# Order of the score tiles on TensorE in the middle batches of a graph-attention and attention kernel

## The chip, the cores and the metric

The kernel runs on one core of a Trainium2 chip. The time is that of one execution on the device, in microseconds (us), and lower is better. A core has five engines that work side by side, each through its own list of instructions in order: TensorE (PE) for matrix products, VectorE (DVE), ScalarE (ACT) and GpSimd (POOL) for elementwise work, and SyncE (SP), which here issues transfers. They wait for each other by semaphores. [...] 

## The reference

For each of 32 batches, x is 512 nodes by 512 features, in fp32, and `adj` is one 512 x 512 mask for all of them. Layer 0 is a graph attention with one head, layer 1 an attention with 8 heads of 64, each with a residual and a layer norm:

```python
def layer0(X, A, W, a):
    h = einsum('bnf,fo->bno', X, W)                    # 512 x 256 a batch
    e = leaky_relu(h @ a[0] + swapaxes(h @ a[1], 1, 2), 0.2)
    alpha = softmax(e + -1e9 * (1 - A), axis=-1)
    return concatenate([einsum('bij,bjo->bio', alpha, h), h], axis=-1)

def layer1(h, adj):
    q, k, v = (split_heads(h @ W.T + b) for W, b in ((Wq, bq), (Wk, bk), (Wv, bv)))
    s = where(adj == 0, -inf, einsum('bhqd,bhkd->bhqk', q, k) / 8)
    out = einsum('bhqk,bhkd->bhqd', softmax(s), v)
    return join_heads(out) @ Wo.T + bo

x = layernorm(x + layer0(x, adj, W, a))
x = layernorm(x + layer1(x, adj))
```

## The kernel before

**Layout.** One batch's 512 rows are four row tiles of 128. The eight heads are four pairs (`hp` 0 to 3); the two heads of a pair share one 128-partition tile of queries and keys, 64 partitions each, so that TensorE works on both at once, on its upper and lower half. All products are in fp32, and the profile shows two matmul records for each. The large projections (queries and keys: `project_two`, tiles `pw`; values: `project_v`, tiles `pv`; output: `finish_seven`, tiles `pf`) are done with seven products of blocks in place of eight, with sums of the blocks made by VectorE or GpSimd.

**A pair.** `head_scores(b, hp, i)` handles row tile i: two score matmuls into two PSUM tiles `ps` (L701); for each of them VectorE adds the mask and takes the row's maximum in one instruction (`minus_max`, L315, result `p` and `least`), and ScalarE takes the exponential and the row sum (L710). `head_blocks` transposes the eight `p` tiles in 32 x 32 blocks on VectorE into `t` (L330), and `head_move` moves blocks with 16 transfers from `t` to `pt` on SP (L347). In the next pair's time `head_products` multiplies `pt` with the values (tile `pav`, L763), and `head_divide` scales by the row sums (`inv`, fetched by GpSimd's transfers in `head_inverse`) into `ot` (L778).

**What runs around it.** While batch b is in its attention, layer 0 of the next batches is woven in. In `middle_batch(b)`, which handles batches 1 to 29:

- pair 0: the values' projection of b (`project_v`, a generator: its first `next` makes product `pv1` and ScalarE's copy of it, L647; the second the other six, three copies and a sum on GpSimd; the end VectorE's four results `v`, L657); layer 0's scores of b+1 (`l0_scores`: ScalarE's leaky rectifier L455, then the mask on GpSimd, L459), its row (`l0_row`, GpSimd L434; `leaky`, VectorE L417) and its weights (`l0_weights`: subtraction on VectorE L469, exponential on ScalarE L470); the first two products of the output projection of b-1 (`finish_seven`).
- pair 1: layer 0's products `po` of b+1 (L477) with their layer norm, then `project_two(b, 1)`: the queries and keys of pairs 2 and 3 (L547, results `qk` on VectorE L584).
- pair 2: the other five products of the output projection (L802).
- pair 3: layer norm of b-1 (`out_stats` on VectorE, `ln_root` on ScalarE, `out_norm` on both), layer 0's projection of b+2 (`l0_project`, four tiles `ph`, L264, copied by ScalarE) and its columns (`l0_columns`: a copy on ScalarE and two transfers on SP, L389 and L391), `l0_maxima` (four reductions on VectorE over `pn`) with two transfers, the store of b-1, and `project_two(b + 1, 0)` for pairs 0 and 1 of the next batch.

**What sets the order.** Each engine runs its instructions in the order in which the Python code records them. PSUM is two pools of four banks: `ps_s` (scores, `psum_s`) and `ps_m` (everything else, `psum`). A new tile takes a bank whose last readers have been recorded, and waits on the chip until they are done. The `p` tiles share nine SBUF buffers with the copies of the projections, `pn` and `row`. Batches 0, 30 and 31 have a loop of their own.

Of the kernel before, what the change touches and what calls it, by code (L numbers as in the profile page):

```python
# [26 lines left out]
def kernel(  # L27
# [241 lines left out]
    def psum_s(name):  # L269
        return ps_s.tile([P, N], F32, name=name, tag="s")  # L270
# [12 lines left out]
    def ln_root(key, tiles=range(NB)):  # L283
        mv, rstd = st["ln", key]
        lo, hi = tiles[0], tiles[-1] + 1
        nc.scalar.activation(rstd[:, lo:hi], mv[:, lo:hi, 1], AF.Sqrt, bias=eps)
# [84 lines left out]
    def l0_project(b, i):  # L371

        l0_copy(b, i, l0_product(b, i))
# [241 lines left out]
    def project_v(b):  # L615

        x1t, tx = st["x1t", b], st["tx", b]
        half = F // 2

        def product(ps, columns, weights, start=True):  # L620
            for k in range(2):
                for c in range(FC // 2):
                    nc.tensor.matmul(  # L623
                        ps[:, k * half : (k + 1) * half],
                        columns(k, c),
                        weights(c),
                        start=start and k == 0 and c == 0,
                        stop=c == FC // 2 - 1,
                        skip_group_check=True,
                    )  # L630

        def a_(i, f):
            cols = slice(i * half, (i + 1) * half)
            return lambda c: wv_sb[:, 2 * f + c, cols]

        def s_(i):
            return lambda c: wvx_sb[:, i, c, :]

        def b_(f, j):
            return lambda k, c: x1t[:, 2 * j + k, 2 * f + c, :]  # L640

        def t_(i):
            return lambda k, c: tx[:, i, k, c, :]

        def copy(ps, name):
            t = prob.tile([P, N], F32, name=f"{name}_{b}_v", tag="p", bufs=PB)
            nc.scalar.copy(t, ps)  # L647
            return t

        out = []  # L650
        for j in range(2):
            v = act.tile([P, 2, F], F32, name=f"v_{b}_{j}", tag="v", bufs=2)
            st["v", b, j] = v
            out.append(v)

        def result(i, j, ps, other):
            nc.vector.tensor_tensor(  # L657
                out[j][:, :, i * half : (i + 1) * half],
                ps.rearrange("p (k d) -> p k d", k=2),
                other.rearrange("p (k d) -> p k d", k=2),  # L660
                ALU.add,
            )

        b1 = psum(f"pv1_{b}")
        product(b1, b_(0, 0), a_(0, 0))
        p1 = copy(b1, "p1")
        yield
        b3, b4 = psum(f"pv3_{b}"), psum(f"pv4_{b}")
        product(b3, t_(0), s_(0))
        p5 = copy(b3, "p5")  # L670
        product(b4, t_(2), a_(1, 0))
        p7 = copy(b4, "p7")
        nc.gpsimd.tensor_tensor(p7, p7, p5, ALU.add)
        product(b1, t_(1), s_(1), start=False)
        u2 = copy(b1, "u2")
        b2 = psum(f"pv2_{b}")
        product(b2, b_(1, 0), a_(0, 1))
        product(b3, b_(1, 1), s_(2), start=False)
        product(b4, t_(3), a_(1, 1), start=False)
        yield  # L680
        result(1, 1, b1, p7)
        result(0, 0, b2, p1)
        result(0, 1, b3, u2)
        result(1, 0, b4, u2)

    def head_scores(b, hp, i):
        qk = st["qk", b, hp]
        if i == 0:
            if (b, hp) not in turned:
                st["t", b, hp] = prob.tile(  # L690
                    [P, 4, 2, FC, NB, G], F32, name=f"t_{b}_{hp}", tag="t", bufs=1
                )
            st["tot", b, hp] = small.tile(
                [P, 2, NB], F32, name=f"tot_{b}_{hp}", tag="total", bufs=3
            )
        total = st["tot", b, hp]
        pss = []
        for j in range(2):
            rows = slice(j * D, (j + 1) * D)
            ps = psum_s(f"ps_{b}_{hp}_{i}_{j}")  # L700
            nc.tensor.matmul(  # L701
                ps, qk[rows, 0, i * P : (i + 1) * P], qk[rows, 1, :], start=True, stop=True
            )
            pss.append(ps)
        for j in range(2):
            name = f"{b}_{hp}_{i}_{j}"
            p = prob.tile([P, N], F32, name=f"p_{name}", tag="p", bufs=PB)
            least = small.tile([P, 1], F32, name=f"least_{name}", tag="least", bufs=6)
            minus_max(p, pss[j], mask1[:, i, :], least)
            nc.scalar.activation(  # L710
                p, p, AF.Exp, bias=least, scale=-1.0, accum_out=total[:, j, i : i + 1]
            )
            st.setdefault(("p", b, hp), []).append((j, i, p))
# [11 lines left out]
    def head_blocks(b, hp):  # L725
        for j, i, p in st.pop(("p", b, hp)):
            transpose_blocks(st["t", b, hp][:, :, j], i, p)
# [29 lines left out]
    def head_products(b, hp, bank=None):  # L757
        pt = st.pop(("pt", b, hp))
        po = st["pav", b, hp] = (bank or psum)(f"pav_{b}_{hp}")
        for c in range(NB):  # L760
            for j in range(2):
                head = 2 * hp + j
                nc.tensor.matmul(  # L763
                    po[j * D : (j + 1) * D, :],
                    st["v", b, c // 2][:, c % 2, head * D : (head + 1) * D],
                    pt[:, :, j, c, :, :].rearrange("p g i q -> p g (i q)"),
                    start=(c == 0),
                    stop=(c == NB - 1),
                )
# [130 lines left out]
    def out_stats(b):  # L900
        z, key = st["x1", b], f"1_{b}"
        for i in range(NB):
            ln_stats(z, key, i)
# [98 lines left out]
    def middle_batch(b):  # L1002


        seven = finish_seven(b - 1, lambda: load_x(b + 1, nc.gpsimd))
        for hp in range(NP):
            last = (b, hp - 1) if hp > 0 else (b - 1, NP - 1)
            head_scores(b, hp, 0)
            head_scores(b, hp, 1)
            if hp in (1, 2):  # L1010
                head_products(*last)
            if hp == 0:
                values = project_v(b)
                next(values)
                l0_scores(b + 1, [0, 1])
            elif hp == 1:
                next(seven)
                l0_add_h(b + 1)
            elif hp == 2:
                add_bias(b + 1)  # L1020
            if hp < 3:
                head_blocks(b, hp)
            else:
                out_stats(b - 1)
                ln_root(f"1_{b - 1}")
                for i in range(NB):
                    l0_project(b + 2, i)
                l0_columns(b + 2)
            head_scores(b, hp, 2)
            head_scores(b, hp, 3)  # L1030
            if hp == 2:
                next(seven)
            else:
                if hp == 3:
                    out_norm(b - 1)
                if hp != 1:
                    head_products(*last)
            pair_ends(b, hp)
            if hp == 2:
                next(seven)  # L1040
            head_divide(*last)
            if hp == 0:
                l0_row(b + 1)
                l0_scores(b + 1, [2, 3])
                leaky(st["row", b + 1])
                next(values)
                l0_weights(b + 1)
                head_inverse(b, 0)
                steps(values)
                next(seven)  # L1050
                next(seven)
            elif hp == 1:
                l0_output(b + 1)
                load_xt(b + 2)
                two = project_two(b, 1)
                next(two)
                l0_norm(b + 1)
                next(two)
                head_inverse(b, 1)
                blocks = x1_blocks(b + 1)  # L1060
                for part in (blocks, two, blocks, two, blocks):
                    next(part, None)
            elif hp == 2:
                steps(seven)
                x1_sums(b + 1, nc.gpsimd)
                head_inverse(b, 2)
                if b == 1:
                    add_bias(1)
            else:
                l0_maxima(b + 2)  # L1070
                l0_write(b + 2)
                l0_read(b + 2)
                store(b - 1)
                steps(project_two(b + 1, 0))
                head_inverse(b, 3)

    before = None
# [201 lines left out]
```

## Time and profile before

| | |
|---|---|
| median of 3 runs | 3063.42 us (3062.69 to 3063.91) |
| span of the profiled execution | 3060.1 us |
| PE, weight load beside it | 99%, 67% busy |
| DVE, ACT, POOL | 84%, 50%, 42% busy |
| DMA | 151 GB/s mean |
| scores L701 | 2048 records, 510.5 us busy |
| products with the values L763 | 2048 records, 467.7 us busy |
| reductions L315 on scores | 1024, mean 683 ns |
| exponentials L710 | 1024, mean 711 ns |
| block transposes L330 | 992, mean 683 ns |

The span covers the first to the last instruction; the runs' time has some microseconds around it. Instructions of one engine overlap at their ends, so the step from one start to the next is what an instruction costs in a run. A batch repeats every 93.6 us: pair 2 of one batch starts its scores at 1506.76 in the trace, that of the next at 1600.39. In that window pair 3 starts at 1523.22, pair 0 at 1550.09 and pair 1 at 1573.45.

### The profile page before, as it was taken

Reading aid. Unit: us, or ns where it says so; the run is one execution under the profiler, and the core shown is the slowest. Engines: PE = TensorE matmul, PEld = TensorE weight load, DVE = VectorE, ACT = ScalarE, POOL = GpSimd, SP = SyncE. Lnnn points to the kernel's source line nnn. Section 1 sums busy time; section 2 is a strip of 40 time slices with the busy share of each in tenths; the row PEclk is TensorE's granted clock in tenths of the full one; section 3 lists DMA queues with packets and bytes.
Section 4 is the critical chain, followed back from the end, with each engine's and each line's share of the span. In section 5 each row is a group of like instructions: output and inputs, shape, how many; then the busy total and the mean of one; then the engine's idle time right before and its main releaser. Section 6 shows DMA issues by size and latency. Waiting matters only on the chain.

```text
span 3060.1 us, 44716 instructions
## 1 busy us (share of the span) xinstructions
PE 3036.1 (99%) x13492; PEld 2061.2 (67%) x13492; DVE 2565.8 (84%) x5707; ACT 1541.0 (50%) x3264; POOL 1287.2 (42%) x1253
## 2 busy tenths in 40 slices
PE   8999999999999999999999999999999999999998
PEld 6666666666666666666666666666666666666665
DVE  7788888888888888888888888888888888888865
ACT  4454555445554545554455545455544555455544
POOL 4353444443434434444444444344444444343422
PEclk9999999999999999999999999999999999999999
DMA  6456666666665666666666666666666666666642
GB/s 185 115 142 162 154 157 155 150 162 156 152 159 144 160 158 154 158 154 147 169 153 149 159 147 162 154 157 151 157 149 164 159 147 163 147 156 159 156 101 66
DMA packets 237440, 462.53 MB, mean 151 GB/s; under 512 B 94544, under 2 KB 97104, under 8 KB 237200
## 3 DMA queue, kind: packets, MB, share of 16 engines
q1 hardware_dynamic: 216848, 395.42, 54.6%
q0 software_dynamic: 20352, 64.25, 6.7%
q8 instruction: 109, 1.79, 0.3%
q14 instruction: 131, 1.07, 0.1%
HBM read 132.65 MB, written 34.27 MB: 55 GB/s over the span
## 4 chain that ended last, share of the span: by engine, by line
PE 92%; DVE 4%; issue 1%; SPq 1%; POOL 1%; DMA 1%; ACT 0%; ACTq 0%; DVEq 0%; POOLq 0%
PE pw L547 23%; PE ps L701 15%; PE pav L763 14%; PE pf L802 12%; PE pv L623 12%; PE ph L264 7%; PE po L477 7%; SPq L347 1%; DVE t L330 1%; DVE p L315 1%; DVE stats L280 0%; PE pt L741 0%; PE pf L876 0%; DVE x L486 0%; ACT p L710 0%
## 5 line engine op out<-in xcount | busy, mean ns | idle before, releaser
L710 ACT ACTIVATE p<-p,least 128x512 f32<-128x512 f32 x1024 | 726.4, 711 | 664.2 <-DVE least L315 629.4
L315 DVE CUSTOM_DVE_ANT_0 p<-ps,mask 128x512 f32<-128x512 f32 x1024 | 642.9, 683 | 129.8 <-PE ps L701 126.4
L330 DVE STREAM_TRANSPOSE t<-p 128x512 f32<-128x512 f32 x992 | 625.6, 683 | 33.8 <-ACT p L710 12.7
L701 PE MATMUL ps<-qk 64*128 64x512 f32 x2048 | 510.5, 615 | 1.4 <-DVE qk L584 1.1
L763 PE MATMUL pav<-pt,v 128*64 128x512 f32 x2048 | 467.7, 598 | 2.6 <-DMA pt<-t 1.9
L754 POOL DMA_DIRECT2D inv<-d_tot x256 | 134.1, 528 | 747.0 <-DMA d_tot<-tot 318.7
L763 PEld LDWEIGHTS pav<-pt,v 128*64 128x64 f32 x2048 | 136.2, 136 | 318.6 <-issue 291.2
L701 PEld LDWEIGHTS ps<-qk 64*128 64x128 f32 x2048 | 177.2, 186 | 236.6 <-issue 161.8
L825 POOL TENSOR_TENSOR x<-x,u_o 128x512 f32<-128x512 f32 x93 | 115.5, 1269 | 338.3 <-ACT u_o L820 338.2
L825 DVE TENSOR_TENSOR x<-x,pf 128x512 f32<-128x512 f32 x186 | 125.4, 677 | 147.9 <-POOL x L825 90.7
L477 PE MATMUL po<-h,et 128*128 128x257 f32 x1024 | 235.1, 386 | 2.6 <-ACT et L470 2.0
L264 PE MATMUL ph<-w_sb,xt 128*128 128x258 f32 x1024 | 234.5, 386 | 0.3 <-DVE w_sb L190 0.3
L600 POOL TENSOR_TENSOR p<-p,p 128x512 f32<-128x512 f32 x64 | 86.5, 1352 | 352.2 <-ACT p L571 352.1
L477 PEld LDWEIGHTS po<-h,et 128*128 128x128 f32 x1024 | 189.1, 190 | 59.8 <-issue 15.8
L264 PEld LDWEIGHTS ph<-w_sb,xt 128*128 128x128 f32 x1024 | 193.0, 191 | 51.2 <-PE ps L701 22.0
L710 ACT ACTIVATION_READ_ACCUMULATOR p<-p,least 128x1 f32 x1024 | 191.4, 187 | 0.0
L710 ACT ACT_TABLE_LOAD x62 | 79.5, 1283 | 210.1 <-DVE least L315 209.6
L459 POOL TENSOR_TENSOR et<-et,mask0t 128x512 f32<-128x512 f32 x126 | 154.6, 1243 | 73.0 <-ACT et L455 72.5
L280 DVE BATCH_NORM_STATS2 stats<-x 128x6 f32<-128x512 f32 x252 | 171.8, 682 | 13.7 <-DVE x L486 0.9
L802 PE MATMUL pf<-wo_sb,ot 128*128 128x256 f32 x744 | 179.6, 384 | 0.1
L802 PE MATMUL pf<-wox_sb,ot 128*128 128x256 f32 x744 | 176.9, 382 | 0.0
L802 PEld LDWEIGHTS pf<-wo_sb,ot 128*128 128x128 f32 x744 | 138.3, 190 | 44.6 <-issue 25.0
(155 smaller groups left out, 5443.9 us busy)
## 6 DMA issues: line engine op xcount, KB each, us to landing
pt<-t SPq DMA_DIRECT2D x1984, 128.0 KB, 2.4
inv<-d_tot POOLq DMA_DIRECT2D x256, 128.0 KB, 3.6
xt<-in_xt_dram SPq DMA_DIRECT2D x31, 1024.0 KB, 7.5
x1t<-x1t_b SPq DMA_DIRECT2D x496, 64.0 KB, 2.0
out_dram<-x SPq DMA_DIRECT2D x31, 1024.0 KB, 6.9
x<-in_x_dram POOLq DMA_DIRECT2D x29, 1024.0 KB, 5.6
rows<-d_att SPq DMA_DIRECT2D x31, 512.0 KB, 3.8
rows<-d_least SPq DMA_DIRECT2D x31, 256.0 KB, 4.3
```

Source lines behind the costliest of these rows:

```text
L264: nc.tensor.matmul(ps, lhs(c), rhs(c), start=(c == 0), stop=(c == FC - 1))
L280: nc.vector.bn_stats(stats, z[:, i, :])
L315: nc.vector.tensor_tensor_reduce(out=out, in0=scores, in1=mask, scale=-1.0, scalar=MIN_INIT, op0=ALU.add, op1=ALU.min, accum_out=least,)
L330: nc.vector.transpose(t[:, :, :, i, :].rearrange("p r c q -> p c r q"), src.rearrange("p (c r k) -> p c r k", r=4, k=G),)
L477: nc.tensor.matmul(po, et[:, j, i * P : (i + 1) * P], h_sb[:, j, 2:], start=(j == 0), stop=(j == NB - 1),)
L547: nc.tensor.matmul(ps[:, k * half : (k + 1) * half], weights(k, c), moving(c), start=start and k == 0 and c == 0, stop=c == FC // 2 - 1, s ...
L623: nc.tensor.matmul(ps[:, k * half : (k + 1) * half], columns(k, c), weights(c), start=start and k == 0 and c == 0, stop=c == FC // 2 - 1, ...
L701: nc.tensor.matmul(ps, qk[rows, 0, i * P : (i + 1) * P], qk[rows, 1, :], start=True, stop=True)
L710: nc.scalar.activation(p, p, AF.Exp, bias=least, scale=-1.0, accum_out=total[:, j, i : i + 1])
L763: nc.tensor.matmul(po[j * D : (j + 1) * D, :], st["v", b, c // 2][:, c % 2, head * D : (head + 1) * D], pt[:, :, j, c, :, :].rearrange("p ...
L802: nc.tensor.matmul(ps[:, k * half : (k + 1) * half], columns[:, c, k * P : (k + 1) * P], weights(c), start=start and k == 0 and c == 0, st ...
L825: engine.tensor_tensor(to, to, term.rearrange("p (k d) -> p k d", k=2), ALU.add)
```

## The change

In the middle batches only. All four row tiles of a pair's scores are recorded in a row; the last two use banks of `ps_m`, and the product with the values of the pair before follows them, in a bank of `ps_s`. All eight block transposes of a pair come together after that (`head_blocks` is left only in `pair_ends`). The values' first product moves behind that product, and layer 0's scores ahead of its copy. Layer 0's projection of b+2 is split: three of its four tiles go to the end of pair 2, behind the output projection, and the fourth stays in pair 3, behind the product with the values, with `l0_columns` after it. The layer norm of b-1 (`out_stats`, `ln_root`, `out_norm`) moves into `project_two(b + 1, 0)`, between its parts, and `l0_maxima` with its transfers too; the store follows.

```diff
-    def head_scores(b, hp, i):
+    def head_scores(b, hp, i, bank=psum_s):
...
-            ps = psum_s(f"ps_{b}_{hp}_{i}_{j}")
+            ps = bank(f"ps_{b}_{hp}_{i}_{j}")
...
-            head_scores(b, hp, 0)
-            head_scores(b, hp, 1)
-            if hp in (1, 2):
-                head_products(*last)
+            for i in range(NB):
+                head_scores(b, hp, i, psum_s if i < 2 else psum)
+            head_products(*last, psum_s)
             if hp == 0:
                 values = project_v(b)
+                l0_scores(b + 1, [0, 1])
                 next(values)
-                l0_scores(b + 1, [0, 1])
             elif hp == 1:
                 next(seven)
                 l0_add_h(b + 1)
             elif hp == 2:
                 add_bias(b + 1)
-            if hp < 3:
-                head_blocks(b, hp)
-            else:
-                out_stats(b - 1)
-                ln_root(f"1_{b - 1}")
-                for i in range(NB):
-                    l0_project(b + 2, i)
-                l0_columns(b + 2)
-            head_scores(b, hp, 2)
-            head_scores(b, hp, 3)
-            if hp == 2:
                 next(seven)
             else:
-                if hp == 3:
-                    out_norm(b - 1)
-                if hp != 1:
-                    head_products(*last)
+                l0_project(b + 2, NB - 1)
+                l0_columns(b + 2)
             pair_ends(b, hp)
...
             elif hp == 2:
                 steps(seven)
+                for i in range(NB - 1):
+                    l0_project(b + 2, i)
                 x1_sums(b + 1, nc.gpsimd)
...
             else:
+                two = project_two(b + 1, 0)
+                out_stats(b - 1)
+                next(two)
+                ln_root(f"1_{b - 1}")
+                out_norm(b - 1)
+                next(two)
                 l0_maxima(b + 2)
                 l0_write(b + 2)
                 l0_read(b + 2)
+                steps(two)
                 store(b - 1)
-                steps(project_two(b + 1, 0))
                 head_inverse(b, 3)
```

## The prediction

> **What bounds the kernel now.** I read the page's busy shares first, then the chain of waits, then the timeline of one middle batch, engine by engine. TensorE is busy nearly all the time, and the chain that ended last is almost wholly TensorE, so only two things count: how long TensorE's own work takes, and any new idle time on it.
>
> ```profile
> PE 3036.1 (99%) x13492; PEld 2061.2 (67%) x13492; DVE 2565.8 (84%) x5707; ACT 1541.0 (50%) x3264; POOL 1287.2 (42%) x1253
> PE 92%; DVE 4%; issue 1%; SPq 1%; POOL 1%; DMA 1%; ACT 0%; ACTq 0%; DVEq 0%; POOLq 0%
> ```
>
> The timeline of TensorE through pair 0 of a batch. Columns: start in us, duration, engine, line, what, count. Let T0 be the start of pair 0's first scores, here 1550.09.
>
> ```profile
> 1550.09 1.99 PE L701 MATMUL ps<-qk 64*128 64x512 f32 x8
> 1552.01 1.99 PE L623 MATMUL pv<-wv_sb,x1t 128*128 128x256 f32 x8
> 1553.93 1.99 PE L701 MATMUL ps<-qk 64*128 64x512 f32 x8
> 1555.85 3.65 PE L763 MATMUL pav<-pt,v 128*64 128x512 f32 x16
> 1561.27 1.89 PE L623 MATMUL pv<-wv_sb,tx 128*128 128x256 f32 x8
> 1562.99 1.89 PE L623 MATMUL pv<-wvx_sb,tx 128*128 128x256 f32 x8
> 1569.90 1.89 PE L802 MATMUL pf<-wo_sb,ot 128*128 128x256 f32 x8
> 1573.45 1.99 PE L701 MATMUL ps<-qk 64*128 64x512 f32 x8
> ```
>
> Eight records of the values' projection take 1.72 us inside a run (1561.27 to 1562.99), but 1.92 us when they stand alone between scores (1552.01 to 1553.93). The array has three shapes here (64*128 scores, 128*64 product, 128*128 the rest), and a run of one shape costs about 0.20 us over its streaming. A score run shows the same: its inner pairs of matmuls start 0.43 apart, so four pairs stream in 1.72, and the run takes 1.92.
>
> The other engines around the same pair:
>
> ```profile
> 1551.99 0.72 ACT L710 ACTIVATE p<-p,least 128x512 f32<-128x512 f32 x1 [6.38 <-DVE least L315]
> 1555.29 2.40 ACT L455 ACTIVATE et<-rows,h 128x512 f32<-128x512 f32 x2
> 1509.01 1.28 ACT L710 ACT_TABLE_LOAD   x1 [6.69 <-DVE least L315]
> ...
> 1556.62 2.31 POOL L459 TENSOR_TENSOR et<-et,mask0t 128x512 f32<-128x512 f32 x2 [0.63 <-ACT et L455]
> 1558.89 2.19 POOL L434 TENSOR_TENSOR row<-rows 128x512 f32<-128x512 f32 x1
> ...
> 1550.60 0.47 DVE L584 SCALAR_TENSOR_TENSOR qk<-pw,bk_sb,u 128x256 f32<-128x256 f32 x1
> 1551.25 0.69 DVE L315 CUSTOM_DVE_ANT_0 p<-ps,mask 128x512 f32<-128x512 f32 x1 [0.18 <-PE ps L701]
> 1562.60 0.83 DVE L417 SCALAR_TENSOR_TENSOR row<-row 128x512 f32<-128x512 f32 x1
> 1563.46 4.41 DVE L469 TENSOR_TENSOR et<-et,row 128x512 f32<-128x512 f32 x4
> 1567.80 1.28 DVE L657 TENSOR_TENSOR v<-pv,p_v 128x512 f32<-128x512 f32 x2
> ```
>
> Look at the order: four exponentials, two leaky rectifiers (L455), two mask additions on POOL, POOL's row (L434), then VectorE's row, four subtractions (L469) and the values' results (L657). The first output-projection matmul (pf, 1569.90) takes the PSUM bank which the first of those results frees, at about 1568.4. This chain has 1.5 us to spare today, and the change lengthens it.
>
> **What the change removes.** Per middle batch the instruction order has 18 runs of one shape before and 12 after: four score runs merge with others, and two full-shape runs (the values' first product, layer 0's projection) join neighbours. 6 x 0.20 = 1.2 us, times 29 middle batches: 34.8 us. The output projection of pair 2 also holds one inner wait today: its 40 records take 1514.17 to 1523.22, 9.05 us, against 40 x 0.2155 + 0.21 = 8.83. It waits for VectorE's addition of the first product, about 12.6 after the pair's start. After the change that addition ends at about 12.05 and is wanted at 12.5, so I take 0.2 more: 1.4 us a batch.
>
> **What it moves, pair 3 (T3 = its first scores).** Nothing is added to any engine, but orders change. TensorE: scores 16 x 0.215 + 0.19 = 3.63, product 3.59 (1555.85 to 1559.43), the last tile of layer 0's projection 1.84, seven products of 1.724 and a switch: the next T0 is T3 + 21.23. The layer norm's root now stands on ScalarE behind the fourth product's copy. That product ends at T3 + 15.96; 0.2 to the copy, copy 0.58, table load 1.28, root 0.30: T3 + 18.3. VectorE is idle meanwhile and has queued behind it: reciprocal and shift 0.58, four results qk 1.80, four reductions of pn at 0.61, four more qk 1.76. It ends at T3 + 24.9, which is T0 + 3.67; today it ends at T0 + 0.98.
>
> **Pair 0, three waits for TensorE.** (a) All four row tiles of scores need eight banks; the last is freed by the last qk, so TensorE waits from T0 + 2.68 to 3.75: 1.05 us. Behind it stand product and projection, which end 1.05 later too. (b) ScalarE: first reduction 3.67, 0.73 later the table load (today pair 0 has none, since the root came in the middle of pair 3; the row of 1509.01 is pair 2's, and it waits for that reduction), 1.30, eight exponentials at 0.704: T0 + 11.33. Two rectifiers 2.29, the copy of the values' first product 0.5: 14.15. TensorE has done three products by 13.55 and may not add to the first bank before the copy: 0.70 us. (c) POOL's two mask additions start 1.33 after the rectifiers, at 12.68, and take 2.27; row 2.19: 17.14. VectorE: row 0.86, subtractions 4.34, first result 0.6: 22.95. TensorE is ready for the output projection at 21.15 and starts at 23.1: 1.95 us. Together 3.7 us a batch. Against the 1.4 saved that is 2.3 us, times 29 = 67 us; the first middle batch enters without the delay of (a), which takes some 2 us off. The profiled execution's span of 3060.1 is 3.3 us under the median of 3063.42; the sum is added to the median: 3128 us.
>
> **What I cost at nothing.** Eight banks filled in 3.6 us while VectorE empties one in 0.61, 4.9 in all: the product's 3.59 us covers that, since the bank next needed is freed by the fifth reduction. Without the cover it would cost 1.3 us a pair. Pairs 1 and 2 find VectorE ready 1.16 and 1.5 after their first scores, as today, and the banks they need free. The 16 moves of pair 3's probabilities stand in SP's queue behind the two transfers of layer 0's columns: those issue about T3 + 12.5 (2.74 after the ACT copy, as today), the moves then run 10.05 us and land about 2.4 later, T0 + 4.05; the product wants them at T0 + 4.7. Pair 2's moves stand behind the 16 of x1t: today they issue from 12.1 to 22.1 after that pair's start and land about 24, and the product of pair 3, which now comes 27.5 after it, will come at 24.9. If either came 1 us later it would cost some 0.1 to 0.35 a batch. The order of the later SP transfers and of POOL is otherwise unchanged.
>
> [...]
>
> **Bounds.** The waits rest on known durations in a known order; errors of 0.3 us in each step of the chain give 2.5 to 4.4 us for their sum, and the saving is 1.0 to 1.6. Net 0.9 to 3.4 us a batch: 3090 to 3160.
>
> **Rivals.** Gain (the other side): the chain through row and results stays hidden. For it: today's 1.5 us of slack and a TensorE that hardly ever waits. Against: the eight exponentials stand ahead of the rectifiers in ScalarE's order. It decides if the first result is done by T0 + 19.4, when an undelayed TensorE wants its bank. Time: 3063.4 - 29 x 1.4 = 3023. Cancelling: VectorE is on time at T0 (the root earlier than I have it), so (a) and (b) vanish and (c) is 22.95 - 2.5 - 19.4 = 1.1, plus 0.2 of latency: 3063 - 29 x 0.1 = 3060. Against: the root cannot run before the fourth product. Worse: 0.20 is paid per two row tiles rather than per run, or the moves land late: 29 x 1 us more, 3157. Against it: the inner pairs of a score run show no such cost.
>
> **How the numbers follow.** Forecast 0.66, gain 0.16, cancelling 0.12, worse 0.06. I predict 3128; its own range is 3090 to 3155. Both signs have weight, but to leave out no more than 2 in 10 the range must take in the cancelling case: 3055 to 3155, which leaves out gain and half of worse. Within 0.2% (6 us, what a measurement of this kernel can tell from no change) lies half of cancelling, 0.06; a quarter of it either side. Faster 0.19, same 0.06, slower 0.75.
>
> **What would show it.** Right: TensorE waits of about 2 us for VectorE's v (L657) before pf, 1 us for qk (L584) in pair 0's scores, 0.7 for the p_v copy; VectorE idle before L417 until POOL's row; a table load after pair 0's first reduction; score runs of 16 records in 3.63 us. Wrong: pf following pv4 without a gap, VectorE's first reduction of pair 0 near T0 + 1.2, or waits in pairs 1 to 3.

## The result and the profile after

The changed kernel takes 3135.16 us (median of 4 runs, 3132.83 to 3139.52) against 3063.06 (4 runs, 3062.29 to 3063.91): the ratio is 1.0238, 95% interval 1.0226 to 1.0251, slower by 72.1 us. The profiled execution took 3134.27 us, its span is 3132.4.

The page of the kernel after, busy shares and the chain of waits:

```profile
PE 3027.1 (97%) x13492; PEld 2100.2 (67%) x13492; DVE 2494.0 (80%) x5707; ACT 1546.6 (49%) x3264; POOL 1284.3 (41%) x1253
...
PE 70%; DVE 12%; POOL 5%; SPq 4%; ACT 3%; issue 3%; DMA 2%; DVEq 0%; ACTq 0%; POOLq 0%
```

TensorE has 9 us less to do and the same number of instructions, yet the span is 72 us longer. Its share of the chain fell from 92% to 70%; VectorE, GpSimd, SyncE and ScalarE took over the rest. Something now stands between TensorE's pieces of work. Here is its timeline through pair 0 of the batch at 1585.49 (T0). Columns: start, duration, engine, line, what, count, and in brackets the idle time before it and what ended that:

```profile
1585.49 4.30 PE L701 MATMUL ps<-qk 64*128 64x512 f32 x16
1590.26 3.65 PE L763 MATMUL pav<-pt,v 128*64 128x512 f32 x16 [0.47 <-DVE least L315]
...
1599.12 1.98 PE L623 MATMUL pv<-wvx_sb,tx 128*128 128x256 f32 x8
...
1604.40 1.89 PE L623 MATMUL pv<-wv_sb,tx 128*128 128x256 f32 x8
1608.67 1.99 PE L802 MATMUL pf<-wo_sb,ot 128*128 128x256 f32 x8 [2.38 <-DVE v L657]
1612.32 3.70 PE L701 MATMUL ps<-qk 64*128 64x512 f32 x16
```

There are three stalls: 0.6 inside the sixteen score records (4.30 for what takes 3.70 in pair 1, the last line), 0.47 before the product, and 2.4 before the output projection pf. The chain of waits of this stretch shows the third. Columns: start, duration, engine and tile, count:

```profile
1596.33 1.14 ACT et L455
...
1597.55 2.28 POOL et L459 x2
1599.83 2.08 POOL row L434
...
1601.94 1.64 DVE row L417
...
1605.06 2.96 DVE et L469 x3
1608.01 0.61 DVE v L657
1608.63 0.04 issue
1608.67 3.72 PE pf L802 x16
```

It is the chain of the prediction: rectifiers, mask additions, row, row, subtractions, first result, and the PSUM bank that it frees for pf. The view of waits of after (engine, tile, line, what it waited for: us in total, times, longest) has this wait 28 times; that of before has no row of it:

```profile
PE pf L802 <- DVE v L657: 65.1, 28, 2.4
```

From TensorE's timeline I took, for each of the 29 middle batches, how long pair 0 lasts (start of its scores to start of pair 1's). In 20 of them it is 26.83 us, whatever the stall before the product is (scores and that stall together take from 4.22 to 5.2, and 3.63 without a stall). **The end of pair 0 is set by one chain on other engines, and the stalls of TensorE on the way to it only share out one delay.** Pairs 1, 2 and 3 last 26.45, 21.28 and 21.25 in most batches: their scores take 3.63.

### The profile page after: what moved, and what is told of

It reads as the page before. It is cut to its first block, busy times and chain, and to the rows that moved or that the text cites. A ratio compares the mean times of both kernels' runs of the same rounds, so it can differ in the third digit from the quotient of the medians.

```text
span 3132.4 us, 44946 instructions
## 1 busy us (share of the span) xinstructions
PE 3027.1 (97%) x13492; PEld 2100.2 (67%) x13492; DVE 2494.0 (80%) x5707; ACT 1546.6 (49%) x3264; POOL 1284.3 (41%) x1253
## 4 chain that ended last, share of the span: by engine, by line
PE 70%; DVE 12%; POOL 5%; SPq 4%; ACT 3%; issue 3%; DMA 2%; DVEq 0%; ACTq 0%; POOLq 0%
PE pw L547 18%; PE pav L763 13%; PE pf L802 11%; PE ps L701 11%; PE po L477 7%; PE ph L264 6%; DVE et L469 4%; PE pv L623 3%; SPq L347 3%; POOL et L459 2%; POOL row L434 2%; DVE qk L584 2%; DVE row L417 1%; SPq L339 1%; DVE junk L315 1%
## 5 line engine op out<-in xcount | busy, mean ns | idle before, releaser
L315 DVE CUSTOM_DVE_ANT_0 p<-ps,mask 128x512 f32<-128x512 f32 x1024 | 635.3, 684 | 159.2 <-PE ps L701 155.8
L330 DVE STREAM_TRANSPOSE t<-p 128x512 f32<-128x512 f32 x992 | 603.3, 674 | 2.2 <-ACT p L710 2.2
L701 PE MATMUL ps<-qk 64*128 64x512 f32 x2048 | 496.8, 605 | 1.4 <-DVE qk L584 1.1
L701 PEld LDWEIGHTS ps<-qk 64*128 64x128 f32 x2048 | 195.3, 186 | 234.5 <-issue 186.6
L802 PE MATMUL pf<-wo_sb,ot 128*128 128x256 f32 x744 | 186.8, 395 | 65.1 <-DVE v L657 65.1
```

The source lines that it names most:

```text
L315: nc.vector.tensor_tensor_reduce(out=out, in0=scores, in1=mask, scale=-1.0, scalar=MIN_INIT, op0=ALU.add, op1=ALU.min, accum_out=least,)
L330: nc.vector.transpose(t[:, :, :, i, :].rearrange("p r c q -> p c r q"), src.rearrange("p (c r k) -> p c r k", r=4, k=G),)
L701: nc.tensor.matmul(ps, qk[rows, 0, i * P : (i + 1) * P], qk[rows, 1, :], start=True, stop=True)
L802: nc.tensor.matmul(ps[:, k * half : (k + 1) * half], columns[:, c, k * P : (k + 1) * P], weights(c), start=start and k == 0 and c == 0, st ...
```

## The experiments

All of them are read by the same number. The table gives, for the kernels that change nothing outside this region, the length of pair 0 that recurs most often (how many of 29 batches are within 0.03 us of it), its mean, and the time that the mean alone gives: 29 x the difference of the means to "after", added to 3135.2.

| kernel | most often (batches) | mean | 29 x difference gives | measured |
|---|---|---|---|---|
| after | 26.83 (20) | 27.09 | | 3135.2 |
| e1_root_early | 23.98 (9) | 24.41 | 3057.5 | 3058.1 |
| e2_row_first | 24.66 (11) | 24.99 | 3074.3 | 3073.6 |
| e3_both | 24.22 (4) | 24.74 | 3067.1 | 3067.0 |
| e4_preload | 25.57 (25) | 25.56 | 3090.8 | 3092.0 |
| e5_root_early_cols_pool | 23.98 (4) | 25.16 | 3079.2 | 3078.1 |
| e6_cols_pool | 26.85 (12) | 27.84 | 3157.0 | 3156.3 |
| e8_root_early_cols_act | 24.00 (15) | 24.20 | 3051.4 | 3050.7 |
| e9_cols_act | 26.83 (15) | 27.34 | 3142.5 | 3143.1 |
| e10_row_first_too | 23.56 (4) | 23.75 | 3038.3 | 3043.6 |
| e11_rectifiers_between | 22.95 (7) | 23.40 | 3028.2 | 3027.7 |
| e12_after_rectifiers_between | 25.24 (21) | 25.22 | 3081.0 | 3081.1 |

These sums miss by at most 1.2 us except for e10, whose profiled execution (3036.51 us, span 3034.7) was the shortest of its four (up to 3046.91). So what these runs differ in lies in pair 0. Each ratio below is to the kernel before, run beside it.

**e1_root_early: the layer norm's statistics and root ahead of pair 3's scores** (in the kernel before they stood between that pair's second and third row tile).

```diff
         for hp in range(NP):
+            if hp == 3:
+                out_stats(b - 1)
+                ln_root(f"1_{b - 1}")
             for i in range(NB):
...
-                out_stats(b - 1)
                 next(two)
-                ln_root(f"1_{b - 1}")
                 out_norm(b - 1)
                 next(two)
```

> The changed kernel with the layer norm's statistics and root of pair 3 put ahead of that pair's scores, so that VectorE finds the root done when it comes to the queries and keys, and the exponential's table is back long before pair 0. Theory (the order on ScalarE makes VectorE late, and the late chain through POOL's row keeps a PSUM bank from the output projection): TensorE's 1.1 us in pair 0's scores vanish, VectorE's first reduction of pair 0 comes about 1.2 us after T0, and the wait before pf falls from 2.5 us to 0.1 to 0.5: 3135 - 29 x 3.3 = about 3040 us. Rival (eight score tiles need all eight banks, and VectorE cannot empty them in time): the wait in the scores stays near 1 us and pf still waits, 3125 to 3135 us.

3058.08 us, ratio 0.9983 (0.9973 to 0.9992). The wait before pf is gone, and with it 77 us. But the wait before the product, which I had put down to VectorE, stayed: scores and wait take 4.93 in the mean against 4.68 after. TensorE's timeline of e1, pair 0:

```profile
1549.89 3.70 PE L701 MATMUL ps<-qk 64*128 64x512 f32 x16
1554.93 3.65 PE L763 MATMUL pav<-pt,v 128*64 128x512 f32 x16 [1.33 <-DVE least L315]
```

The scores run through in 3.70, so the banks come free in time and VectorE is not late. The product waits 1.33 all the same. The releaser in brackets had long been done at that moment; the chain of waits names the true one, the last of 16 moves of pair 3's probabilities:

```profile
1550.16 0.59 SPq L347
...
1550.80 3.70 DMA pt<-t
1554.50 0.42 issue
1554.93 3.65 PE pav L763 x16
```

And the queue of SyncE in e1 shows why they are late:

```profile
1540.52 0.33 SPq L391 DMA_DIRECT2D rows<-d_att  x1
1541.09 10.31 SPq L347 DMA_DIRECT2D pt<-t  x16
```

VectorE had begun the eight transposes at 1534.70 and ended them at 1539.5; the moves stood in the queue behind the transfer of layer 0's columns (L391), which itself starts 2 us behind the transfer before it (1538.55). They cost nothing in after, where pair 0 is set later by the chain, and became the bound once that chain was short.

**e2_row_first: only GpSimd's row ahead of the mask additions.**

```diff
                 values = project_v(b)
+                l0_row(b + 1)
                 l0_scores(b + 1, [0, 1])
...
-                l0_row(b + 1)
                 l0_scores(b + 1, [2, 3])
```

> The changed kernel with POOL's row (L434) recorded ahead of the mask additions of pair 0 instead of behind the first two. Theory: the row is done by T0 + 11.5, VectorE goes on right after its division at about T0 + 13.8, the first result is ready by T0 + 20.5 and pf does not wait any more, while the 1.1 us in pair 0's scores stay: 3135 - 29 x 2.5 = about 3062 us. Rival (the bank is late because VectorE as a whole is late, not because of POOL's order): no more than 0.5 us a batch is won, 3120 to 3135 us.

3073.57 us, ratio 1.0033 (1.0021 to 1.0045): 62 us of the 72 come back although root, table load and rectifiers stay where they are. Two mask additions less ahead of the row are 2.28 us by the chain above, and pair 0 went from 26.83 to 24.66, 2.17 less. It fell short of the expectation because the moves then decide in some batches (scores and wait up to 6.13).

**e3_both: e1 and e2 together.**

> Both edits together: the root ahead of pair 3's scores and POOL's row ahead of the mask additions. Theory: no wait of pair 0 is left, and the merged runs show their worth, 12 runs a batch in place of 18 at 0.2 us each and the inner wait of the output projection gone: 92.2 to 92.7 us a batch against 93.6 before, 3022 to 3038 us. Rival (the moves of pair 3 behind the columns' two transfers are late by themselves): the product with the values waits for pt in pair 0, up to 0.5 us a batch, and the time is 3040 to 3050 us. Rival (merging runs saves nothing): 3060 us or more.

3066.97 us, ratio 1.0011 (1.0002 to 1.0021): a miss, and slower than e1. By its time alone it would fit the second rival, that merging saves nothing; e7 and e11 below speak against that one. The view of waits of e3 has a new line:

```profile
POOL row L434 <- DMA rows<-d_least: 39.9, 12, 4.5
```

Ahead of everything else on GpSimd, the row waits for the transfer of layer 0's maxima, and holds the mask additions behind it.

**e4_preload: after, and a 128x1 exponential behind the layer norm, whose result nobody uses, so that the table of exponentials is loaded before pair 0's first reduction is there.**

```diff
                 out_norm(b - 1)
+                warm = small.tile([P, 1], F32, name=f"warm_{b}", tag="warm", bufs=1)
+                nc.scalar.activation(warm, eps, AF.Exp)
                 next(two)
```

> The changed kernel with one exponential of a 128 x 1 tile (its result unused) behind the layer norm's last scaling in pair 3, so that the exponential's table is loaded while ScalarE has nothing to do. Theory: pair 0's exponentials start 1.28 us earlier and with them the rectifiers, POOL's additions and the row: the wait before pf falls by about 1.2 us, the 1.1 us in the scores stay: 3135 - 29 x 1.25 = about 3099 us. Rival (VectorE's own lateness decides, or the load is hidden): 3130 to 3137 us.

3091.99 us, ratio 1.0094 (1.0077 to 1.0111). ScalarE's timeline, after first, then e4:

```profile
1589.28 1.28 ACT L710 ACT_TABLE_LOAD   x1 [3.30 <-issue]
```

```profile
1471.20 1.28 ACT L1064 ACT_TABLE_LOAD   x1
1472.50 0.20 ACT L1064 ACTIVATE warm<-eps 128x1 f32<-128x1 f32 x1
1474.50 0.72 ACT L710 ACTIVATE p<-p,least 128x512 f32<-128x512 f32 x1 [1.80 <-issue]
```

After, the load comes when its instruction is due, although ScalarE has been idle for 3.30; in e4 it lies in that idle time. Pair 0 goes from 26.83 to 25.57: 1.26 for a load of 1.28. The table load was wholly on the chain. 29 x 1.26 are 37 of the 43 us gained; most of the rest is the clock, below, which in e4 is never halved in these batches.

**e5_root_early_cols_pool and e6_cols_pool: layer 0's two column transfers on GpSimd's queue**, in e1 and in after, so that the moves on SyncE's queue are free of them.

```diff
-    def l0_columns(b):
+    def l0_columns(b, queue=nc.sync):
...
-        nc.sync.dma_start(d.rearrange("k p i -> p k i"), att)
+        queue.dma_start(d.rearrange("k p i -> p k i"), att)
...
-        nc.sync.dma_start(rows, d.partition_broadcast(P))
+        queue.dma_start(rows, d.partition_broadcast(P))
...
-                l0_columns(b + 2)
+                l0_columns(b + 2, nc.gpsimd)
```

> The kernel with the root ahead of pair 3's scores (e1), and the two transfers of layer 0's columns issued by GpSimd in place of SP, so that pair 3's 16 moves start when the transposes are done. In e1 TensorE waits 1.3 us a batch before pair 0's product, while the moves, issued from 1541.1 behind the columns, still land. Theory (the moves stand 1.6 us behind the columns): the wait falls below 0.3 us, a batch takes 92.2 to 92.6 us, 3058 - 29 x 1.2 = about 3022 us. Rival (the product waits for VectorE's first reduction, or the moves take longer whenever they start): the wait stays above 1 us, 3050 to 3060 us.

> The changed kernel with the columns' two transfers on GpSimd's queue and nothing else. Theory: in the changed kernel the wait before pair 0's product has two causes at once, VectorE's late queries and keys (0.5 us) and the late moves (the rest to 1.1), so it falls to about 0.5 us; but the output projection's start is set by the chain from VectorE's late first reduction through exponentials, rectifiers, POOL and results, which does not begin with the product, so what the first wait gives back the second takes: 3130 to 3138 us, with the full run of pair 0 some 0.5 us longer. Rival (the waits add up): 3135 - 29 x 0.5 = about 3120 us.

e5: 3078.10 us, ratio 1.0048 (1.0033 to 1.0063). e6: 3156.34, ratio 1.0297 (1.0282 to 1.0313). Both are misses on the wrong side. The broadcast rows land later from this queue (the views of transfers of e1 and of e5: line, queue, count, size, median us from issue to landing): counted from pair 3's start 1.5 us later in the median. In e5 GpSimd's `pn` waits 60.3 us for them (19.9 in e1), and VectorE's reductions wait for `pn`, which in e1 cost 1.2 us in all:

```profile
rows<-d_att SPq DMA_DIRECT2D x31, 512.0 KB, 5.0
```

```profile
rows<-d_att POOLq DMA_DIRECT2D x29, 512.0 KB, 6.0
...
DVE junk L315 <- POOL pn L404: 34.8, 22, 3.2
```

Those reductions stand ahead of the last `qk`, and with the chain behind them late again, TensorE waits 32.4 us for pf (0.2 in e1).

**e7_before_six_runs: the price of a run, by itself.** The kernel before, with a product of two columns on 64 partitions between the four tiles of layer 0's projection: three a batch for 29 batches. Each cuts a run of one shape in two; their results are not used.

```diff
     def l0_product(b, i):
...
+        if 3 <= b and i < NB - 1:
+            nc.tensor.matmul(
+                bank[:, 384:386], wv_sb[:D, 0, :P], wv_sb[:D, 0, :2], start=True, stop=True
+            )
```

> The kernel before with three more runs of the array's other shape in each of 29 batches: behind three of the four tiles of layer 0's projection one 64-row matmul of two columns (its result unused), which adds six runs a batch, as many as the change takes away. Theory (a run of one shape costs 0.20 us wherever it stands): 29 x 6 x 0.20 = 35 us and the three tiny matmuls' own time, 0.05 to 0.2 us each, 4 to 17 us: 3102 to 3115 us. Rival (the 0.20 us belongs to long runs, or is what the weight load costs once): under 3085 us.

3106.90 us, ratio 1.0137 (1.0120 to 1.0154): 42.3 us over the 3064.62 of the kernel before beside it, 1.46 a batch. TensorE's timeline:

```profile
1547.22 2.01 PE L264 MATMUL ph<-w_sb,xt 128*128 128x258 f32 x8
1549.16 0.38 PE L364 MATMUL ph<-wv_sb 64*128 64x2 f32 x2
1549.47 2.01 PE L264 MATMUL ph<-w_sb,xt 128*128 128x258 f32 x8
```

From start to start a tile now takes 1.94 where it takes 1.74 inside a run ((7.18 - 0.20) / 4 for the four tiles of before, 1525.13 to 1532.31), and the product of two columns takes 0.31, though its records stream four columns. Three times 0.31 and three times 0.20 are 1.53. A tile that stands behind a cut pays the 0.20 in full, as read off the timeline of before; how much of the small product's 0.31 is its own time and how much the price of its run, this run doesn't separate; the 0.05 to 0.2 us expected for it alone was an estimate that no run shows. What TensorE does in the 0.20 is not shown either: it is a price for this kernel's shapes.

**e8_root_early_cols_act and e9_cols_act: the same transfers on ScalarE's queue**, right behind the copy that makes their data (the diff of e5 with `nc.scalar`), in e1 and in after.

> The kernel with the root ahead of pair 3's scores, and the columns' two transfers issued by ScalarE, which has nothing to do between its last copy of layer 0's projection and the first of the queries and keys. On GpSimd's queue the rows landed 4 us later than on SP's and VectorE's reductions over them became the late piece; from ScalarE they should be issued at the same time as from SP. Theory (what e1 still waits for is 1.6 us of SP's queue behind the columns): pair 3's moves start with the end of the transposes, the wait before pair 0's product falls from 1.3 to under 0.5 us, no wait before pf comes back: 3025 to 3036 us. Rival (the moves are bound by the transfers' own time and the traffic beside them): the wait stays at 0.9 us or more, 3045 to 3060 us.

> The changed kernel with the columns' two transfers on ScalarE's queue and nothing else. Theory: the first wait of pair 0 has two causes side by side, VectorE late by its order (which alone leaves 0.5 us) and the late moves, so it falls from 1.1 to about 0.5 us; the start of the output projection is set by the chain that begins with VectorE's first reduction, not with the product, so the wait before pf grows by as much: 3130 to 3138 us. Rival (the waits add up): 3112 to 3122 us.

The "4 us later" of the first text is too much; it was 1.5, as said under e5. e8: 3050.68 us, ratio 0.9958 (0.9942 to 0.9975), in the rival's range, though not by the rival's mechanism. SyncE's queue of e8, where the transposes ended at 1536.1 (eight of them from 1531.25, 4.86 us):

```profile
1536.18 10.70 SPq L347 DMA_DIRECT2D pt<-t  x16
```

The moves now issue as soon as their data is there. Scores and wait take 4.10 in the mean against e1's 4.93, but in 15 batches pair 0 lasts 24.00, as it did in 9 of e1's, and pf waits again:

```profile
PE pf L802 <- DVE v L657: 15.8, 24, 1.3
```

The time won before the product was paid back at pf: under the moves' bound lay the chain's, 1.05 above the 22.95 of a pair 0 without waits (e11, below).

e9: 3143.07 us, ratio 1.0260 (1.0245 to 1.0275). I had expected no gain, and there is none, but it is 5 us above my range. The moves are early, scores and wait take 4.45 for 4.68, and pair 0 lasts 26.83 as before it, in 15 batches. **This is the plainest of the runs: a wait of TensorE was made shorter, and nothing came of it, because the end was set elsewhere.** Part of why it is 8 us longer than after is told below, under the clock.

**e10_row_first_too: e8 and the row first.**

> The root ahead of pair 3's scores, the columns on ScalarE's queue, and POOL's row ahead of the mask additions. In e8 TensorE still waits 0.8 us a batch before pf and 0.4 before pair 0's product. Theory (the row stands behind two mask additions on POOL): the row is done 2 to 3 us earlier, VectorE goes on after its division, the wait before pf falls under 0.2 us: 3051 - 29 x 0.7 = about 3030 us. Rival (the row cannot start before the transfer of layer 0's minima has landed, about T0 + 8.5 or later, and now holds the mask additions up, which is what made e3 slower than e1): no gain, 3045 to 3060 us, with POOL's row waiting on that transfer.

3043.61 us, ratio 0.9928 (0.9913 to 0.9944), between theory and rival. It gains some 7 us on e8 and loses part of what it gains as e3 did: GpSimd's row waits for the maxima.

```profile
POOL row L434 <- DMA rows<-d_least: 53.2, 13, 12.3
```

**e11_rectifiers_between and e12_after_rectifiers_between: pair 0's two rectifiers between the second and third row tile of scores, as before**, in e8 and in after. ScalarE then has them behind four exponentials, not eight.

```diff
             for i in range(NB):
                 head_scores(b, hp, i, psum_s if i < 2 else psum)
+                if hp == 0 and i == 1:
+                    l0_scores(b + 1, [0, 1])
             head_products(*last, psum_s)
             if hp == 0:
                 values = project_v(b)
-                l0_scores(b + 1, [0, 1])
                 next(values)
```

> The root ahead of pair 3's scores, the columns on ScalarE's queue, and pair 0's first two rectifiers after four exponentials instead of eight, where they stand in the kernel before; the matmuls keep the changed kernel's order. Theory (ScalarE's order makes the row late): mask additions and row come 2.8 us earlier without waiting for anything else, no wait before pf is left, 3051 - 29 x 0.8 = about 3027 us; what is left against 92.1 us a batch is the wait of pairs 0 and 3 for the moves, 0.4 and 0.15 us. Rival (the last four exponentials, 2.3 us later, make the transposes and the next moves late): 3045 us or more, with a longer wait before pair 1's product.

> The changed kernel with pair 0's first two rectifiers after four exponentials instead of eight and nothing else. Theory: of the prediction's third wait nothing or almost nothing is left, while the first (1.1 us in pair 0's scores) stays: 3135 - 29 x 2.3 = about 3068 us. Rival (the wait before pf comes from VectorE's late start and the table load, whatever stands behind the exponentials): 3110 to 3135 us.

e11: **3027.71 us (3025.63 to 3030.32), ratio 0.9880 (0.9863 to 0.9896): 36 us below the kernel before, with the merged runs kept**, and what the theory had. Its page:

```profile
PE 2987.9 (99%) x13492; PEld 2089.5 (69%) x13492; DVE 2494.6 (82%) x5707; ACT 1545.0 (51%) x3264; POOL 1289.2 (43%) x1253
```

TensorE never waits for pf, and pair 0 lasts 22.95 where the moves are in time. In the mean it lasts 23.40; what is left is the wait for the moves:

```profile
1626.73 3.70 PE L701 MATMUL ps<-qk 64*128 64x512 f32 x16
1631.62 3.65 PE L763 MATMUL pav<-pt,v 128*64 128x512 f32 x16 [1.19 <-DMA d_least<-least]
```

That line of e11's timeline is one of its longer waits. The transfer in brackets is a later one of the same queue; the last of the 16 moves had issued at 1626.46 and landed at 1631.21. With pair 3's wait (21.42 in the mean, 21.25 without) it comes to 0.45 + 0.17 = 0.62 a batch, 18 us. A kernel without it was not tried.

e12: 3081.07 us, ratio 1.0055 (1.0040 to 1.0070). Pair 0 lasts 25.24 in 21 batches, 1.59 less than after: the rectifiers' place is worth that much with root and table load left late. I had expected some 13 us more of it. Four exponentials are 2.8, but GpSimd's row is now done before VectorE, with its own transposes and a division in front, reaches L417 (1479.85, GpSimd's row ended at 1478.74), and the four subtractions behind it take 5.38, where they took 4.41 in the kernel before; GpSimd's additions and sum run beside them, and whether those are the cause was not tested.

## Why the prediction was right

I predicted 3128 us, from a gain of 1.4 and a loss of 3.7 a batch; the kernel takes 3135. Sign, mechanism and chain were right; that the sum came so close is in part luck. Point by point:

**The saving, 1.4 a batch.** A batch without waits, put together from the lengths above (pair 0's from e11), takes 22.95 + 26.45 + 21.28 + 21.25 = 91.93 against 93.64: 1.71. Six runs at 0.20 fit, as e7 priced them, and so does the inner wait of pair 2's output projection, which is gone. 0.3 more lie in pair 1, in small pauses within its last run: layer 0's products go from 7.17 to 7.05 us and queries and keys from 12.37 to 12.18 (medians of TensorE's timelines). What made those pauses I did not trace.

**(a) 1.05 before the product.** The size is right (4.68 - 3.63 = 1.05 in the mean), the cause only in part. VectorE's first reduction comes at T0 + 3.04, not 3.67:

```profile
1588.13 0.48 DVE L584 SCALAR_TENSOR_TENSOR qk<-pw,bk_sb,u 128x256 f32<-128x256 f32 x1
1588.53 0.68 DVE L315 CUSTOM_DVE_ANT_0 p<-ps,mask 128x512 f32<-128x512 f32 x1
```

That leaves 0.6 of scores late, the 4.30 of the timeline, and no batch of after has less (scores and wait take 4.22 at least). What comes on top, up to 5.36, is the moves, which I had landing at T0 + 4.05 and **costed at nothing**. In this batch the last one issued at T0 + 1.24 and landed at T0 + 4.57, 3.3 us later where I had taken 2.4, and the product started 0.2 after that; in 24 of the 29 batches the product waits for that landing and follows it by 0.13 to 0.50. With VectorE on time (e1) the wait was still there; with the moves early (e9) at least 0.6 was. So 1.05 came out by luck, from two causes of which I had priced one, and that one too high. In after neither of these waits of TensorE cost time by itself, since both lie in front of the later end; VectorE's late start counts because the chain begins with it.

**(b) 0.70 for the copy of `pv1`.** It was about 0.1: the exponentials ended at T0 + 10.74 and not 11.33, and the copy came nearly in time (the tile at 1599.12 takes 1.83 to the next start, its neighbours 1.73).

**(c) 1.95 before pf, and the end of it all.** The first result was to be done at T0 + 22.95, pf to start at T0 + 23.1; pf started at T0 + 23.18 (1608.67). TensorE was there earlier than I thought, since (b) was missing, so the wait itself is 2.4. But two errors cancel in the chain, which is luck. It came to GpSimd's first mask addition 0.6 early (T0 + 12.06 for 12.68), and then **VectorE's row, which I put at 0.86, took 1.63**:

```profile
1601.86 2.72 POOL L459 TENSOR_TENSOR et<-et,mask0t 128x512 f32<-128x512 f32 x2
```

```profile
1601.94 1.63 DVE L417 SCALAR_TENSOR_TENSOR row<-row 128x512 f32<-128x512 f32 x1 [2.62 <-POOL row L434]
```

GpSimd goes from its row straight to the next mask addition, 0.08 us before VectorE starts. In the kernel before that addition began at 1561.72 and L417 ended at 1563.43; after, 1601.86 and 1603.57; in e11, 1639.21 and 1640.92. In all three L417 ends 1.71 after GpSimd's start, while its duration is 0.83, 1.63 and 1.15, and the addition takes 1.16: it ends as if it waited for the addition and then needed some 0.6 (its shortest in these traces is 0.64). In e12 the two start 0.03 apart, and there it is GpSimd's side that is longer: its two additions take 3.29 together for 2.72 in after, and L417 0.68.

```profile
1479.82 3.29 POOL L459 TENSOR_TENSOR et<-et,mask0t 128x512 f32<-128x512 f32 x2 [1.08 <-ACT et L455]
```

```profile
1479.85 0.68 DVE L417 SCALAR_TENSOR_TENSOR row<-row 128x512 f32<-128x512 f32 x1
```

In the first three kernels GpSimd starts first and VectorE's instruction is the longer for it, in e12 GpSimd's are; that one holds the other up is my reading of these times. What they would contend for is not shown, and no run takes the addition out of the way by itself. My price came from a row that had met the addition half-way through.

**Sum and size.** Pair 0 was forecast to last 23.1 and then 3.65 for the two output tiles, 26.75; it lasts 26.83 in 20 of 29 batches. Against 22.95 that is a loss of 3.9 a batch for the 3.7. Net 3.9 - 1.7 = 2.2, times 29 = 63 us. The first middle batch, whose pair 0 lasts 23.79, takes 3 off (I had some 2). The small waits of pair 3, 0.12 a batch, add 3.5; they are the step "the product of pair 3 will come at 24.9", where pair 2's moves are sometimes later. The rest, 10 us, is a term that the prediction lacked altogether: the clock, below. Together 73.5, against 72.1 measured.

**The rivals.** Gain: its condition was the first result by T0 + 19.4; it came at 23.1. e11 fulfils that condition by two moves of instructions and one of transfers, and takes 3027.7, close to the rival's 3023. Cancelling: VectorE on time at T0 is e1, 3058 for the rival's 3060, but by luck: there (a) did not vanish and (c) did, the reverse of what the rival had. Worse: its price per two row tiles is refuted by 3.63 us for sixteen score records in pairs 1 and 2; its late moves came true in part, but in pair 0 they lay in front of the later end, and in pair 3 they cost 0.12. The same number bears out what was costed at nothing: eight banks, emptied at 0.61 each under the product's 3.59, never held TensorE there.

## What to carry to other kernels

When a chain over four engines ends in a buffer that the bottleneck needs, work out when it ends, not how long each of the bottleneck's waits is: waits in front of a fixed end don't add, and removing one of them gives nothing (e9: scores and wait 4.45 for 4.68, pair 0 26.83 in most batches of both). To merge runs on TensorE was worth its 0.20 us a run here, but every instruction that has stood between the pieces (here two rectifiers, a square root, two transfers) keeps its due time: look first whether it can stay between the same instructions of its own engine as before, whatever TensorE's order becomes. A table load that waits for its instruction's operand can be drawn forward by an instruction without operands to wait for (e4: 1.26 us of a load of 1.28).

## What the runs showed of the hardware

**TensorE's clock halved after some 2 us of idle time, when they fell within one stretch of 3.41 us.** In 6 of the 29 batches of after pair 0 lasts 28.5 instead of 26.83. The windows view of after, TensorE's columns first; PEclk, the granted clock, is the third number from the end:

```profile
1504.00:1509.00 5.00, 4.80 (x23) 3.88 (x21) 4.45 (x3) 1.90 (x4) 4.76 (x4) 1.00 0.90 203
1509.00:1511.20 2.20, 0.02 (x1) 0.03 (x1) 2.20 (x5) 1.83 (x3) 0.00 (x0) 1.00 0.93 210
...
1512.00:1515.00 3.00, 3.00 (x9) 2.38 (x8) 1.60 (x3) 0.00 (x0) 0.22 (x1) 0.50 0.09 10
...
1516.50:1520.00 3.50, 3.50 (x17) 1.46 (x16) 3.02 (x8) 1.59 (x5) 3.40 (x4) 1.00 0.59 152
```

TensorE had idled for the usual 2.4 us before pf; then the clock stood at 0.50 for about 3.4 us, and the sixteen records of pf took 5.33 instead of 3.65, 1.68 more. Six times 1.68 are 10 us, the missing term. It happened 12 times in e6 and 8 times in e9, which accounts for 10 of e6's 21 us over after and for 3 of e9's 8; the rest are batches in which the chain itself is later, by something that I did not trace. In e4, whose waits before pf are 1.2 us in the mean (31.3 in 27), the mean granted clock of the span is 1.000; it is 0.996 in after and 0.993 in e6.

Which of the equal waits are hit is not chance. The traces record the granted clock with its times: within after, and within e6 and e9, the half-rate stretches in the middle of the kernel last 3.41 us each and start on a grid of 3.413 us (549.39, 1126.24, 1511.95 in after: 169 and 113 steps apart). In all 26 of them, at least 1.89 us of the wait before pf lay within the one grid step that ended as the clock fell; of the other 58 waits over 1 us in these three kernels, none had more than 1.90 in one step. So a wait of 2.4 went free where the grid cut it in two. What sets the grid, and what decides on the half rate, these traces do not show beyond that.

**The same 512 KB broadcast landed latest from GpSimd's queue**: 4.7 us after its issue from SyncE's queue in after and 5.0 in e1, 5.2 from ScalarE's in e8 and 5.3 in e10 and e11, 6.0 from GpSimd's in e5 (medians). On SyncE's queue itself it took 3.8 in before, so one queue's own spread (1.2) is as large as the distance between the queues (1.0), and ScalarE's difference is not shown to be the queue's.
